# Attention rows scaled per head on ScalarE, GpSimd's joins and bias accumulations reordered, one Strassen level for one item's last factor

## The chip, the core and the metric

The kernel runs on one core of one Trainium2 chip. The metric is the device time of one execution in microseconds (us), and the value compared is the median of several runs. A profiled execution of the kernel before gives the timings by instruction; all times below that are not run times count from the start of its span.

The core has a matrix engine (TensorE, PE in the profile), three engines for elementwise work (VectorE = DVE, ScalarE = ACT, GpSimd = POOL) and a queue engine for transfers (SyncE = SP). Each engine works through its own instructions in order, and engines wait for each other by semaphores.

## What is computed

For each of 32 items `b`, with 512 nodes and 512 features, in float32:

```python
q, k, v = x @ Wq + bq, x @ Wk + bk, x @ Wv + bv          # 8 heads of 64
w       = softmax(q k^T / 8 + mask(adj))
x1      = layernorm(x + w v)
z       = norm_adj @ x1                                   # D^-1/2 adj D^-1/2
out     = layernorm(x1 + z @ W1 + b1)
```

The softmax is computed without subtracting the maximum, so that the division by the row sums can be made late: `yT` first holds the undivided `w v`, and is then multiplied, head by head, by `inv`, the reciprocal of the row sums.

## The kernel before, in words

**Tiling.** A node or feature axis of 512 is four tiles of 128 partitions. The products with the 512x512 weights are Strassen products: seven half-size products in place of eight. In most items, four of the seven are replaced by one more level, seven quarter-size products (`quarters_of`, called `leaf`), and the three others are `OUTER`. `seven` runs a table of products; every product accumulates in a PSUM region (A, B or D) and is moved out of it by a `put` or an `add` at the named steps. A later product into the same region has to wait until the earlier content has been read. In the leaf, `put` is a ScalarE copy and `add` a VectorE addition. For the attention's values, the target is tile `v`; for the graph convolution's second factor it is `y`.

**One item.** An iteration of the loop over `b` (line 874) runs four stages, and TensorE goes from one to the next without a gap in the program:

1. `stretch(b, one)`: scores, exponentials and value products of the first two head pairs. The 8 score tiles of 128x1024 use four PSUM pairs in turn, VectorE masks and moves each out (`e<-sc,maskT`), ScalarE takes the exponential, GpSimd adds the four tiles of a pair of heads to `acc` (`accumulate`). The value product of a pair is transposed by VectorE into the single buffer `yb`, and four SP transfers of 64 KB carry `yb` to `yT` (`unload_values`).
2. keys and queries of item `b+1` (`k0`, `k1`: 14 products). Beside it VectorE, ScalarE and GpSimd finish the convolution of item `b-2` and normalize item `b-1` (`measure`, `root`, `norm`, `low`).
3. `stretch(b, two)`: the other two head pairs.
4. A list of 27 pieces called `main` in line 949, numbered 0 to 26, for b from 1 to LAST-1 = 30: first factor of the convolution of item `b-1` (0 to 3), the leaf of the values of item `b+1` (4 to 10) and its `spread_last` (11), one outer product of the convolution (12), two steps of the outer products of the values (13), the leaf of the convolution (14 to 20), one outer step without a product (21), `spread_last` of `y` (22), and two outer products of each in turn (23 to 26).

**Order.** `play(main, beside)` writes out by hand which helper work follows which piece. All four compute engines keep that program order (`InOrder`); SP's transfers are not pinned. So a helper on an engine that waits holds all that is behind it there.

**Names that the change touches.** `inverse` makes `inv`; `scale` (line 606) is one VectorE multiplication of 128x512 per node tile with a broadcast `inv`; `grow` (668) multiplies the normalized rows of item `b-1` by `rdeg` on ScalarE; `combined` (779), called `join`, adds these rows to `y` on GpSimd; `residual` and `residual_bias` (673, 677) are GpSimd DMAs that add `x[b]` and `bv` to `yT`, 1 MB each; `lift` (664) adds `b1`; `second` (835) is the convolution's second factor with one level, seven half-size products, all moved out by VectorE. `stored[2]` holds `w1` in DRAM as it is before the quarter-size weights are written into it. `extend` is left for the last but one convolution.

Of the kernel before, what the change touches and what calls it, by code (L numbers as in the profile page):

```python
# [14 lines left out]
AF = mybir.ActivationFunctionType  # L15
# [4 lines left out]
H = 8  # L20
HD = 64
# [29 lines left out]
def unshifted(  # L51
# [14 lines left out]
    nc = tc.nc  # L66
# [32 lines left out]
    def each(f, *args):  # L99
        return [lambda a=a: f(*a) if isinstance(a, tuple) else f(a) for a in args]  # L100

    def run(pieces):
        for f in pieces:
            f()
# [155 lines left out]
    def swap(k):  # L260
        nc.sync.dma_start(wqv, stored[k])
# [202 lines left out]
    def accumulate(b, g):  # L464
        e = E[b, g]
        if b < LAST:
            a = work.tile([P, 2, N], F32, name="acc", bufs=2)
            gpsimd.tensor_add(a, e[0], e[1])
            for j in range(2, NT):
                gpsimd.tensor_add(a, a, e[j])  # L470
            ACC[b, g] = [a]
            return
        ACC[b, g] = []
        for l in range(2):
            n = 2 * ORDER.index(g) + l
            if n < 2:
                a = work.tile([P, 2, N], F32, name="acc", bufs=2)
            else:
                t, at = ((XT, 0), (XT, 2), (XT, 4), (wqv, 0), (wqv, 2), (wqv, 4))[n - 2]
                a = t[:, at : at + 2].rearrange("p k u o -> p k (u o)")  # L480
            gpsimd.tensor_add(a, e[2 * l], e[2 * l + 1])
            ACC[b, g].append(a)
# [26 lines left out]
                yb[32 * q : 32 * (q + 1)],  # L509
            )  # L510

    def stretch(b, gs, gap=()):
        banks("attention")
        for g in gs:
            scores(b, g)
        for g in gs:
            accumulate(b, g)
        banks("products")
        for g in gs:
            av = bank([P, N], "av")  # L520
            values(b, g, av)
            unload_values(b, g, av)
            if g == gs[0]:
                run(gap)
# [47 lines left out]
    def finish(b):  # L572
# [33 lines left out]
        def scale(i):  # L606
# [3 lines left out]
                t["inv"][:, i, :, None].to_broadcast([P, H, HD]),  # L610
            )

        def add(i):
            gpsimd.tensor_add(YT[b][:, i, :], YT[b][:, i, :], R[b][i])

# [57 lines left out]
        def residual():  # L673
# [7 lines left out]
            turn_values=[lambda: turn_values(ORDER[-1], bank([P, N]))],  # L681
            pairs=[[lambda i=i, g=g: add_pair(i, g) for i in all_] for g in ORDER],
            halves=each(root, (0, 2), (2, 2)),
            inverse=[inverse_all], scale=each(scale, *all_), add=each(add, *behind),
            measure=each(measure, *(all_ if b == LAST else behind)), root=[root],
            judge=[judge], norm=each(norm, *all_), low=each(low, *all_),
            lift=each(lift, *((3, 0, 1, 2) if b == LAST else behind)),
            grow=each(grow, *(all_ if b == LAST else behind)),
        )

    def convolve(b):
# [127 lines left out]
        def store(n, at):  # L819
# [11 lines left out]
            first=each(first, *range(DT)), block=each(block, *nodes), unload=each(unload, *range(DT)),  # L831
            parts=each(combine, *range(4)), quarters=each(quarter, *range(4)),
            leaf=quarters_of(left, w1, w1_quarters, lambda: t["whole"], begin), spread_last=spread_last,
            outer=seven(OUTER, multiply, put, add), join=each(combined, (0, 1), (1, 1), (0, 0), (1, 0)),
            second=seven(LATE_LOW if last else CHAIN, multiply, put, add), extend=extend,
            halves=[each(measure_half, *((n, i) for n in range(2))) for i in range(2)],
            measure=each(measure, *nodes), root=each(root, (0, NT)), store=each(store, *((n, 0) for n in nodes)),
# [36 lines left out]
    for b in range(B):  # L874
        one, two = ORDER[:2], ORDER[2:]
        f[b], c[b] = finish(b), convolve(b)
        ahead, back = f.get(b - 1), c.get(b - 2)
        if b == LAST:
            load_residual(b)
        stretch(b, one, (ahead["low"] if b == LAST else []) + (back["measure"][:3] if back else []))  # L880

        def folds(gs):
            return [[lambda g=g, b=b: fold(b, g)] for g in gs]

        def turns(b=b + 2):
            if b >= B:
                return [], [], []
            return [lambda: turn(b, 0)], [lambda: turn(b, 1)], [lambda k=k: combine(b, k) for k in range(4)]

        fold0, fold1 = folds(one) if b < LAST else ([], [])  # L890
        rest = back["measure"][3:] + back["root"] if back else []
        store = back["store"] if back else []
        if b < LAST:
            k0, k1 = keys_and_queries(b + 1, 0), keys_and_queries(b + 1, 1)
            main = [p for pair in zip(k0, k1) for p in pair]
            if b == 0:
                exact = each(compare, *range(NT))
                weights = each(lambda k: weigh_part(w1, gpsimd, k), *range(4))
                beside = {
                    1: fold0, 2: [degrees], 3: weights[:1], 4: fold1, 5: weights[1:2] + exact[:1], 6: exact[1:2],  # L900
                    7: weights[2:3], 8: exact[2:3], 9: weights[3:], 10: exact[3:], 11: [quarters],
                    12: each(lambda k: weigh_quarter(w1, w1_quarters, k, gpsimd), *range(3)),
                }
            else:
                measure, norm, low = ahead["measure"], ahead["norm"], ahead["low"]
                scale = ahead["inverse"] + ahead["scale"] if b == 1 else []
                beside = {
                    0: rest + scale + (ahead["add"] if b == 1 else []), 1: store[:1] + fold0, 2: store[1:2], 3: store[2:3] + fold1,
                    4: store[3:] + measure[:2], 5: measure[2:] + ahead["root"] + [quarters], 7: norm[:1] + ahead["judge"],
                    8: norm[1:2] + low[:1], 9: norm[2:3] + low[1:2], 10: norm[3:] + low[2:3],  # L910
                    11: low[3:] + ahead["lift_all"],
                }
            play(main, beside)
            if b == 0:
                nc.sync.dma_start(stored[2], w1)
        else:
            e = f[b]
            conv = c[b - 1]
            play(conv["first"], {
                0: rest + store[:1] + conv["parts"][:0], 1: store[1:2] + ahead["judge"] + conv["parts"][:1],  # L920
                2: store[2:] + e["sums0"],
                3: conv["parts"][1:] + e["inverse0"] + ahead["lift"] + ahead["grow"],
            })

        if b < LAST:
            swap(1)
        if b == LAST - 1:
            load_residual(b)
        stretch(b, two, f[b]["pairs"][0] + f[b]["pairs"][1] if b == LAST else ())

        fold0, fold1 = folds(two) if b < LAST else ([], [])
        turn0, turn1, combined = turns()
        if b + 2 < B:
            load_x(b + 2, 0)
            load_x(b + 2, 1)
        if b < LAST:
            end = f[b]
            leaf, spread_last, outer = values_of(b + 1)
            main = leaf + [spread_last]
            if b == 0:  # L940
                main += [lambda: run(outer[:2])] + outer[2:]
                play(main, {
                    1: fold0, 4: fold1, 8: turn0, 9: turn1 + combined[:2] + [lambda: weigh_quarter(w1, w1_quarters, 3, gpsimd)],
                    10: combined[2:] + [lambda: swap(0)],
                })
            else:
                conv = c[b - 1]
                other, join = conv["outer"], conv["join"]
                main = (
                    conv["first"] + main + other[:1] + [lambda: run(outer[:2])] + conv["leaf"] + other[1:2]  # L950
                    + [conv["spread_last"]] + outer[2:3] + other[2:3] + outer[3:] + other[3:]
                )
                grow, scale = ahead["grow"], end["scale"]
                parts = conv["parts"] + conv["quarters"]
                if b < LAST - 1:
                    beside = {
                        1: parts[:1] + fold0, 3: parts[1:] + fold1, 5: end["inverse"], 9: scale[:1], 10: scale[1:3],
                        12: scale[3:] + grow, 13: turn0 + turn1 + end["residual"] + combined[:1], 22: join[:1], 23: join[1:2],
                        24: join[2:3] + combined[1:2], 25: join[3:] + combined[2:], 26: end["residual_bias"] + [lambda: swap(0)],
                    }  # L960
                else:
                    measure, norm = end["measure"], end["norm"]
                    beside = {
                        1: parts[:1] + fold0, 3: parts[1:] + fold1, 5: end["inverse"], 9: scale[3:], 10: scale[:2],
                        12: scale[2:3] + grow + end["add"], 21: measure[:2], 22: join[:1], 23: join[1:2] + measure[2:] + end["root"],
                        24: join[2:3] + norm[:2], 25: join[3:] + norm[2:3],
                        26: norm[3:] + [lambda: nc.sync.dma_start(w1, stored[2])],
                    }
                play(main, beside)

# [311 lines left out]
```

## Time and profile before

| | |
|---|---|
| median of 3 runs | 2805.27 us (2803.79 to 2805.3) |
| the profiled execution's own time | 2805.72 us |
| its span, from first to last instruction | 2803.7 us, mean granted TensorE clock 0.997 |
| busy share of the span | PE 97%, DVE 76%, POOL 74%, ACT 47% |
| chain of work that ended last, by engine | PE 89%, DVE 8%, issue 2% |

One item in the middle of the run, from one start of stage 1 to the next, is 86.0 us. Its stages, with the time in each that the engines were busy:

| stage | from, to (us) | length | PE | DVE | ACT | POOL |
|---|---|---|---|---|---|---|
| 1, scores | 1322.80, 1330.70 | 7.90 | 7.83 | 7.15 | 4.30 | 7.47 |
| 1, values | 1330.70, 1337.80 | 7.10 | 7.07 | 6.27 | 4.14 | 6.94 |
| 2 | 1337.80, 1362.10 | 24.30 | 24.30 | 20.01 | 14.17 | 14.58 |
| 3 | 1362.10, 1376.20 | 14.10 | 14.10 | 9.86 | 9.30 | 9.21 |
| 4, pieces 0 to 3 | 1376.20, 1383.60 | 7.40 | 7.40 | 5.24 | 1.77 | 6.26 |
| 4, pieces 4 to 11 | 1383.60, 1390.40 | 6.80 | 6.80 | 3.78 | 2.35 | 5.64 |
| 4, pieces 12, 13 | 1390.40, 1393.85 | 3.45 | 3.45 | 3.45 | 3.04 | 3.37 |
| 4, pieces 14 to 20 | 1393.85, 1400.86 | 7.01 | 5.74 | 7.01 | 1.76 | 4.73 |
| 4, pieces 20 to 26 | 1400.86, 1408.83 | 7.97 | 7.97 | 3.80 | 0.59 | 6.17 |

A line of the timeline has the start, the length, the engine, the source line (L45 is the helper that records every pinned operation, so the tile names tell the work), the operation with output and inputs, the shape, the count, and in brackets the idle time of the engine before it and what ended that. `w` is `w1` and `w_quarters` its quarter-size parts; `e` is also the buffer in which the first factor of the convolution lies. For groups of instructions, times are means of single instructions; such a time includes latency, so back-to-back instructions of one kind can start at a shorter distance than their length.

### The profile page before, as it was taken

The numbers are of one execution on the slowest core, as the hardware profiler recorded it, in microseconds if no ns is written. First come the engines' busy times: TensorE is split into PE (matmuls) and PEld (weight loads), VectorE is DVE, ScalarE is ACT, GpSimd is POOL, SyncE is SP. The second block draws the span as 40 slices with busy tenths as digits, with TensorE's granted clock in tenths as the row PEclk, the third lists the DMA queues.
The fourth block names the chain that finished last, engine by engine and source line by source line (L and its number), as shares of the span: only waits on it lengthen the run. The fifth ranks groups of instructions, "written<-read, shape, count | busy, mean of one in ns | idle before, by whom it ended". The sixth has DMA issues, their size and how long they took to land.

```text
span 2803.7 us, 38312 instructions
## 1 busy us (share of the span) xinstructions
PE 2731.0 (97%) x14004; PEld 1929.7 (69%) x14004; DVE 2130.2 (76%) x2809; ACT 1329.1 (47%) x1927; POOL 2062.0 (74%) x1336
## 2 busy tenths in 40 slices
PE   9999999999999999999999999999999999999997
PEld 6677676676676766767767767667677676676664
DVE  4787777777877777777778777778777777777866
ACT  3345444445544454444554444554445444445543
POOL 5777767767777777777777777777867767767765
PEclk9999999999999999999999999999999999999998
DMA  6344545545445445454454554554544545545541
GB/s 181 112 106 102 130 101 135 119 103 129 118 104 124 113 113 124 100 132 122 100 134 108 119 123 100 128 123 100 127 121 102 130 100 135 121 102 129 132 106 35
DMA packets 419684, 325.30 MB, mean 116 GB/s; under 512 B 278432, under 2 KB 346016, under 8 KB 411168
## 3 DMA queue, kind: packets, MB, share of 16 engines
q1 hardware_dynamic: 370432, 226.04, 26.6%
q0 software_dynamic: 48048, 95.43, 21.6%
q8 instruction: 113, 1.85, 0.3%
q10 hardware_dynamic: 1008, 1.31, 0.2%
q14 instruction: 83, 0.68, 0.1%
HBM read 250.35 MB, written 39.06 MB: 103 GB/s over the span
## 4 chain that ended last, share of the span: by engine, by line
PE 89%; DVE 8%; issue 2%; POOL 0%; DMA 0%; ACT 0%; SPq 0%; DVEq 0%; POOLq 0%; ACTq 0%
PE mm L45 56%; PE sc L45 17%; PE av L45 16%; DVE yT L45 3%; DVE xT L45 2%; DVE y L45 1%; DVE v L45 1%; DMA yT<-yb 0%; DVE st L45 0%; DVE lo L45 0%; POOL yT L45 0%; DVE yb L45 0%; DMA xr<-in_x_dram 0%; ACT xT L45 0%; SPq L507 0%
## 5 line engine op out<-in xcount | busy, mean ns | idle before, releaser
L45 ACT ACTIVATE e<-e 128x1024 f32<-128x1024 f32 x512 | 539.5, 1057 | 369.1 <-DVE e L45 339.1
L45 DVE SCALAR_TENSOR_TENSOR e<-sc,maskT 128x1024 f32<-128x1024 f32 x512 | 585.0, 1216 | 90.8 <-PE sc L45 90.7
L45 POOL TENSOR_TENSOR acc<-acc,e 128x1024 f32<-128x1024 f32 x248 | 589.2, 2376 | 19.4
L45 PE MATMUL sc<-kq 64*128 64x512 f32 x2048 | 478.7, 605 | 0.5 <-ACT zT L45 0.4
L45 PE MATMUL av<-e,v 128*64 128x512 f32 x2048 | 456.2, 597 | 7.3 <-ACT e L45 4.3
L45 PE MATMUL mm<-xT,wk 128*128 128x256 f32 x1792 | 463.1, 381 | 0.0
L45 PE MATMUL mm<-xT,wqv 128*128 128x256 f32 x1792 | 459.9, 379 | 0.0
L45 POOL TENSOR_TENSOR acc<-e 128x1024 f32<-128x1024 f32 x126 | 297.0, 2357 | 156.4 <-ACT e L45 156.4
L45 POOL TENSOR_TENSOR xT<-xT 128x512 f32<-128x512 f32 x251 | 346.1, 1389 | 77.4 <-PE mm L45 41.1
L45 POOL TENSOR_TENSOR e<-e 128x512 f32<-128x512 f32 x244 | 331.6, 1370 | 75.5 <-ACT e L45 57.3
L45 PEld LDWEIGHTS mm<-xT,wk 128*128 128x128 f32 x1792 | 337.6, 190 | 69.8 <-DVE mv L45 23.5
L45 PEld LDWEIGHTS mm<-xT,wqv 128*128 128x128 f32 x1792 | 340.5, 190 | 46.3
L45 PEld LDWEIGHTS sc<-kq 64*128 64x128 f32 x2048 | 184.7, 186 | 262.6 <-issue 142.0
L45 PEld LDWEIGHTS av<-e,v 128*64 128x64 f32 x2048 | 158.3, 137 | 299.8 <-issue 223.9
L45 ACT ACTIVATE kq<-mm,bias 128x256 f32<-128x256 f32 x512 | 214.7, 473 | 288.9 <-PE mm L45 277.1
L45 PE MATMUL mm<-w,e 128*128 128x128 f32 (+1 forms) x1680 | 299.1, 321 | 37.3 <-DVE y L45 36.8
L45 PE MATMUL mm<-wqv,xT 128*128 128x128 f32 x1736 | 309.4, 322 | 2.5 <-DVE v L45 2.4
L45 PEld LDWEIGHTS mm<-w,e 128*128 128x128 f32 x1680 | 252.8, 191 | 61.6 <-issue 41.5
L45 DVE STREAM_TRANSPOSE yb<-av 128x512 f32<-128x512 f32 x127 | 91.1, 717 | 267.2 <-DMA yT<-yb 184.5
L45 PEld LDWEIGHTS mm<-wqv,xT 128*128 128x128 f32 x1736 | 262.2, 192 | 28.7 <-DVE v L45 3.1
L45 POOL TENSOR_TENSOR rstd<-ve,minus_half 128x4 f32<-128x4 f32 (+1 forms) x66 | 66.1, 1002 | 233.7 <-DVE nmu L45 230.8
L45 DVE TENSOR_TENSOR v<-v,mm 128x512 f32<-128x512 f32 x221 | 148.6, 685 | 83.6 <-PE mm L45 83.4
(140 smaller groups left out, 3523.1 us busy)
## 6 DMA issues: line engine op xcount, KB each, us to landing
wqv<-wv_parts SPq DMA_DIRECT2D x31, 1792.0 KB, 11.9
wqv<-wq_parts SPq DMA_DIRECT2D x30, 1792.0 KB, 7.1
yT<-yb SPq DMA_DIRECT2D x508, 64.0 KB, 2.4
e<-in_x_dram SPq DMA_DIRECT2D x248, 128.0 KB, 2.6
yT<-in_L_gnn_bias_dram POOLq DMA_DIRECT2D x30, 1024.0 KB, 14.5
out_dram<-y SPq DMA_DIRECT2D x120, 256.0 KB, 2.0
yT<-in_x_dram POOLq DMA_DIRECT2D x29, 1024.0 KB, 9.2
yT<-in_L_gnn_bv_dram POOLq DMA_DIRECT2D x29, 1024.0 KB, 9.5
```

The lines of the kernel that those rows point to most:

```text
L45: return self.tc.keep_in_program_order(op(*args, **kwargs))
```

## The change

- In items 1 to 29, the four VectorE multiplications of `scale` become 32 ScalarE activations of 128x64 (`scale_head`), placed in groups of 10, 10, 9 and 3 after pieces 6, 10, 16 and 20. `grow` moves from piece 12 to piece 20.
- In the same items, the GpSimd transfer `residual` moves from piece 13 to piece 22, and `residual_bias` from piece 26 to the next item's first stretch, between `accumulate` of its first and second head pair. The joins go in the order (0,0), (1,0), (1,1), (0,1) in place of (0,1), (1,1), (0,0), (1,0), the last of them after piece 24 in place of 25.
- In item 30, stage 4 computes the second factor of item 29's convolution with one level: `second` in place of leaf, outer products, `quarters`, `spread_last` and joins. Its list has 22 pieces. `w1` is read back from DRAM before stage 3 in place of after piece 26. `scale` (still on VectorE), `grow`, `add`, `measure`, `root` and `norm` of item 30 come earlier, and `low` and `lift` move into this list from the first stretch and from piece 3 of item 31.

```diff
-    def stretch(b, gs, gap=()):
+    def stretch(b, gs, gap=(), between=()):
...
         for g in gs:
             accumulate(b, g)
+            if g == gs[0]:
+                run(between)
...
+        def scale_head(i, h):
+            y = YT[b][:, i, ts(h, HD)]
+            scalar.activation(y, y, AF.Copy, scale=t["inv"][:, i, h : h + 1])
...
-            inverse=[inverse_all], scale=each(scale, *all_), add=each(add, *behind),
+            inverse=[inverse_all], scale=each(scale, *all_),
+            scale_heads=each(scale_head, *((i, h) for i in all_ for h in range(H))), add=each(add, *behind),
...
-            grow=each(grow, *(all_ if b == LAST else behind)),
+            grow=each(grow, *all_),
...
-            join=each(combined, (0, 1), (1, 1), (0, 0), (1, 0)),
+            join=each(combined, (0, 0), (1, 0), (1, 1), (0, 1)),
...
-        stretch(b, one, (ahead["low"] if b == LAST else []) + (back["measure"][:3] if back else []))
+        between = ahead["residual_bias"] if 1 < b < LAST else []
+        stretch(b, one, back["measure"][:3] if back else (), between)
...
-                3: conv["parts"][1:] + e["inverse0"] + ahead["lift"] + ahead["grow"],
+                3: conv["parts"][1:] + e["inverse0"] + ahead["grow"],
...
         if b == LAST - 1:
             load_residual(b)
+            nc.sync.dma_start(w1, stored[2])
         stretch(b, two, f[b]["pairs"][0] + f[b]["pairs"][1] if b == LAST else ())
...
+                if b < LAST - 1:
+                    main = (
...
                    )
+                else:
+                    second = conv["second"]
+                    main = (
+                        conv["first"] + main + second[:1] + [lambda: run(outer[:2])] + second[1:2] + outer[2:3]
+                        + second[2:3] + outer[3:] + second[3:]
+                    )
                 grow, scale = ahead["grow"], end["scale"]
-                parts = conv["parts"] + conv["quarters"]
+                parts, heads = conv["parts"], end["scale_heads"]
                 if b < LAST - 1:
                     beside = {
-                        1: parts[:1] + fold0, 3: parts[1:] + fold1, 5: end["inverse"], 9: scale[:1], 10: scale[1:3],
-                        12: scale[3:] + grow, 13: turn0 + turn1 + end["residual"] + combined[:1], 22: join[:1], 23: join[1:2],
-                        24: join[2:3] + combined[1:2], 25: join[3:] + combined[2:], 26: end["residual_bias"] + [lambda: swap(0)],
+                        1: parts[:1] + fold0, 3: parts[1:] + conv["quarters"] + fold1, 5: end["inverse"], 6: heads[:10], 10: heads[10:20],
+                        13: turn0 + turn1 + combined[:1], 16: heads[20:29], 20: heads[29:] + grow,
+                        22: end["residual"] + join[:1], 23: join[1:2],
+                        24: join[2:] + combined[1:2], 25: combined[2:], 26: [lambda: swap(0)],
                     }
                 else:
-                    measure, norm = end["measure"], end["norm"]
+                    measure, norm, low = end["measure"], end["norm"], end["low"]
                     beside = {
-                        1: parts[:1] + fold0, 3: parts[1:] + fold1, 5: end["inverse"], 9: scale[3:], 10: scale[:2],
-                        12: scale[2:3] + grow + end["add"], 21: measure[:2], 22: join[:1], 23: join[1:2] + measure[2:] + end["root"],
-                        24: join[2:3] + norm[:2], 25: join[3:] + norm[2:3],
-                        26: norm[3:] + [lambda: nc.sync.dma_start(w1, stored[2])],
+                        1: parts[:1] + fold0, 3: parts[1:] + fold1, 5: end["inverse"], 6: grow[:1],
+                        8: grow[1:2] + scale[3:], 9: grow[2:3] + scale[:1], 10: grow[3:] + scale[1:3] + end["add"],
+                        14: measure[:2], 15: measure[2:3], 16: measure[3:] + end["root"],
+                        17: norm[:1], 18: norm[1:2] + low[:1], 19: norm[2:3] + low[1:2],
+                        20: norm[3:] + low[2:3], 21: low[3:] + end["lift"],
                     }
```

More of the change, by code (lines that the diff above doesn't have):

```diff
@@ L833, in convolve @@
             leaf=quarters_of(left, w1, w1_quarters, lambda: t["whole"], begin), spread_last=spread_last,
-            outer=seven(OUTER, multiply, put, add), join=each(combined, (0, 1), (1, 1), (0, 0), (1, 0)),
+            outer=seven(OUTER, multiply, put, add), join=each(combined, (0, 0), (1, 0), (1, 1), (0, 1)),
             second=seven(LATE_LOW if last else CHAIN, multiply, put, add), extend=extend,
@@ L948, in unshifted @@
                 other, join = conv["outer"], conv["join"]
[L949 to L952, printed above, removed]
+                if b < LAST - 1:
+                    main = (
+                        conv["first"] + main + other[:1] + [lambda: run(outer[:2])] + conv["leaf"] + other[1:2]
+                        + [conv["spread_last"]] + outer[2:3] + other[2:3] + outer[3:] + other[3:]
+                    )
[4 more added lines that the diff above has]
+                        + second[2:3] + outer[3:] + second[3:]
+                    )
```

## The prediction

> **What bounds the kernel now.** TensorE is busy for 97% of the span (2731.0 of 2803.7 us), and 89% of the chain that ended last is PE. So only TensorE's gaps, and work slowed by late inputs, can be won. I read its waits first:
>
> ```profile
> PE mm L45 <- DVE y L45: 36.8, 29, 1.3
> ...
> PE av L45 <- ACT e L45: 4.3, 1, 4.3
> ```
>
> (total us, times, longest.) Half of the span's 72.7 us without PE is one wait of 1.27 us in each of 29 items. Its place, in TensorE's timeline of one item:
>
> ```profile
> 1398.53 1.06 PE L45 MATMUL mm<-w,e 128*128 128x128 f32 x8
> 1400.86 1.13 PE L45 MATMUL mm<-w,e 128*128 128x128 f32 x8 [1.27 <-DVE y L45]
> ```
>
> This is piece 20, the convolution leaf's last product; its PSUM region must first be read by VectorE. VectorE's timeline there:
>
> ```profile
> 1389.48 0.69 DVE L45 TENSOR_TENSOR v<-v,mm 128x512 f32<-128x512 f32 x1 [0.20 <-PE mm L45]
> 1390.09 6.58 DVE L45 TENSOR_TENSOR yT<-yT,inv 128x512 f32<-128x512 f32 x4
> 1396.59 0.68 DVE L45 TENSOR_TENSOR v<-v,mm 128x512 f32<-128x512 f32 x1
> 1397.19 2.36 DVE L45 STREAM_TRANSPOSE xT<-e 128x1024 f32<-128x1024 f32 x2
> 1399.48 1.84 DVE L45 TENSOR_TENSOR y<-y,mm 128x512 f32<-128x512 f32 x3
> ```
>
> The four scale multiplications hold everything up: the addition to `v` whose product was done at about 1394.0, the two transposes, and the additions to `y`.
>
> Next, the two score stretches of an item, which do equal work, and what VectorE does before the first:
>
> ```profile
> 1322.81 7.82 PE L45 MATMUL sc<-kq 64*128 64x512 f32 x32
> 1362.12 7.14 PE L45 MATMUL sc<-kq 64*128 64x512 f32 x32
> ```
> ```profile
> 1410.27 0.69 DVE L45 TENSOR_TENSOR y<-y,mm 128x512 f32<-128x512 f32 x1 [0.57 <-POOL y L45]
> ```
>
> From the scores' start to the value products it is 7.92 us (1322.81 to 1330.73) against 7.07 (1362.12 to 1369.19). The first stretch's masking starts 2.03 us after its scores (1322.81 to 1324.84), the second's 1.17 (1363.29), and the last score tiles wait for a PSUM pair. VectorE is late because its last addition waits for GpSimd's last join.
>
> Last, the end of the program:
>
> ```profile
> 2719.94 0.50 PE L45 MATMUL mm<-adjT,lo 128*128 128x512 f32 x1 [1.40 <-DVE lo L45]
> 2741.82 9.68 PE L45 MATMUL av<-e,v 128*64 128x512 f32 x32 [4.35 <-ACT e L45]
> ```
> ```profile
> 2735.09 4.97 POOL L45 TENSOR_TENSOR yT<-yT,b_r 128x512 f32<-128x512 f32 x4
> ```
>
> Item 31's exponentials lie on ScalarE behind `grow`, which waits for GpSimd's `lift`; before that, TensorE waited for `low`.
>
> [...] The scale rows agree: minimum 678 ns, median 1755 with GpSimd at work. I go by the trace's 6.5 us per item for what VectorE is freed of. [...] The one place where `yb` meets a bias accumulation agrees: eight transfers land in 2.3/4.1/7.1 us (least, median, most; item 30, 2650 to 2682), against 2.4 elsewhere:
>
> ```profile
> 2655.47 1.28 POOL L45 DMA_DIRECT2D wk<-in_L_gnn_bv_dram  x1 [3.04 <-PE sc L45]
> ```
> ```profile
> 2672.28 0.72 DVE L45 STREAM_TRANSPOSE yb<-av 128x512 f32<-128x512 f32 x1 [8.15 <-DMA yT<-yb]
> ```
>
> **The change, part by part.**
>
> *Scale on ScalarE (items 1 to 29).* Removed from VectorE: 6.5 us. The addition to `v` can then run at 1394.1 and the transposes end at 1397.1; the additions to `y` follow their products (ends near 1397.6, 1398.5, 1399.4), as those to `v` do in the other leaf without any PE wait. **The 1.27 us go: 29 x 1.27 = 36.8 us.**
>
> Added: 32 activations of 128x64. No row shows this shape. Four `grow` of 128x512 take 2.56 us and one 0.713, so they start 0.62 apart; two `kq` of 128x256 take 0.84 and one 0.473, 0.37 apart. That is 0.25 us and 1 ns per column, so 64 columns come every 0.19 to 0.3 us; without any overlap it would be 0.41 (0.713 less 448 columns at 0.67 ns, from the 1057 ns of 1024 columns). I take 0.29: groups of 2.9, 2.9, 2.6 and 0.9 us. The gaps in ScalarE's timeline: `inv` is ready at 1387.1 and the next copy due at 1390.6 (3.3 us); then until 1394.9 (3.8 us, freed of `grow`'s 2.56); from 1397.4 until about 1400.6 (3.2 us). All fit, so cost nothing. At 0.41 each group overruns, by up to 0.9 us.
>
> `grow` at piece 20 ends about 2.7 us before the next scores; join (0,0) needs its first two tiles, done 4.0 before.
>
> *Joins and `residual`.* Counted from the next scores' start, GpSimd's `y<-y` ends at -4.9 (1403.96, scores at 1408.83). Then `residual` (1.3) and four joins of 1.24: (1,1) ends at +0.1, (1,0) at -1.1. VectorE's last two additions, at piece 26, need these two and not the fourth join; their product ends at about +0.1. They run from +0.2 to +1.4, masking starts at +1.4 in place of +2.03. A PSUM pair is free three and four masks of 1.14 later, so the last tile waits no longer: **7.92 becomes 7.15, 29 x 0.77 = 22.3 us.** If GpSimd is a microsecond later, this gain is lost, no more.
>
> *`residual_bias` in the stretch.* GpSimd's `acc` then runs from +5.1 to +12.3, the DMA is issued until +13.6, and the second `acc` ends at +20.9 (20.0 before). Behind it wait `rstd` of item b-2, ScalarE's normalizations, and the copies of keys and queries between them. Its packets begin 2.4 us after issue (1326.72, DMA busy from 1329.1), at +14.7. The four `yb` transfers move from +12.8 to +15.8, so the fourth collides. Alternating with the 5.4 us of the accumulation it lands at about +20.5; `yb` is reused then, in place of +17.0. VectorE gets 1.3 us back, since the addition `ve` (1.51 us beside GpSimd's `acc`, 0.17 elsewhere) then runs alone: `nmu` is +22.5 in place of +20.1. With TensorE 0.77 earlier, ScalarE's copies are 3.2 us later against the pieces of stage 2; the ninth piece needs the copy that ended at 1348.68 and started at 1351.66, 3.0 us of cover. **I charge 0.3 us per item, 8.7 us**; bounds: 0, if the transfers just miss each other, and 1.8, if `yb` is a little later and `ve` no shorter. `residual` and `swap(0)` now overlap, as `lift_all` and `swap(1)` do (14.5 and 11.9 us to landing); used at +12.3 and +14.9, landed by about +9.6 and +10.4: nothing.
>
> *Items 30 and 31.* One level: ten pieces of 1.73 us in place of six (10.4) and a leaf of 6.55, +0.4 us on TensorE. GpSimd saves quarters and joins. Item 31 loses the `low` waits (1.4 and some 0.9 of pauses behind it), and its exponentials start behind `grow` alone, at about 2730.5. Value products then begin right after the scores, which are 2.3 earlier, and take 7.1: end near 2742 in place of 2751.5. **Gain 9.5**; I take 8, as VectorE is fuller in item 30. `w1`'s transfer is off the path if SP issues it when `w1` is free (about 2613); if it lies before `yb` in the queue it costs up to 6. I charge 1. Net 7.
>
> Sum: 36.8 + 22.3 - 8.7 + 7 = 57.4. The span becomes 2746.3, with the 2.0 us around it (2805.72 - 2803.7) 2748.3; that execution was 0.45 above the median shown, so **2748**.
>
> **Rivals.**
> 1. *No collision and all gains*, 36.8 + 22.3 + 9.5 = 68.6: 2737. For it: the overlap is only about a microsecond. Chance 0.20.
> 2. *ScalarE becomes the late one*: 0.41 us per head delays a copy that frees the leaf's first region, 0.9 us per item, and the joins. Gain 0.4 + 0.4 per item, 29 x 0.8 + 7 = 30: 2775. Against it: every shape of the trace overlaps its neighbour by 0.1 us. Chance 0.12.
> 3. *Slower*: the accumulation takes `yb`'s place as the bound of stage 2. It decides once `yb` frees later than about +22.6: of each us of delay over the 3.0 of cover TensorE loses one, and at 5.3 of delay (+20.5 is 3.2) the 2.04 us won per item and the 7 at the end, 0.24 per item, are gone. At a stall of 2.6 per item: 29 x (2.04 - 2.6) + 7 = -9: 2814. For it: item 30 shows `yb` held 8.15 us and TensorE stalled 1.9 behind it. Against: three transfers were in flight there. Chance 0.10.
>
> Forecast's own case 0.58, 2742 to 2765. **Range 2735 to 2785**: it takes in rivals 1 and 2 and a collision of up to 1 us per item. About 0.2% (5.6 us) is what can be told from no change: faster 0.88, within it 0.02, slower 0.10.
>
> **What would show it.** PE's wait for DVE `y` gone from its waits; the first score stretch at 7.1 to 7.2 us; no `av<-e` wait near the end; heads starting under 0.3 us apart; landing of `yT<-yb` with a maximum near 7 us in most items. A PE wait for ACT `kq` of over 2 us in stage 2 would make the prediction wrong, and so would a new wait for ACT `y` in the leaf.

## The result and the profile after

The changed kernel takes 2849.93 us (median of 6 runs, 2844.58 to 2858.17) against 2804.25 us for the kernel before (6 runs): a ratio of 1.0164, 95% interval 1.0145 to 1.0183. It is slower by 1.6%, where 2% faster was forecast.

The profiled execution took 2853.71 us. First the wait of TensorE that is largest in total (total us, times, longest), then the span and the granted clock, which was 0.997 before:

```profile
PE mm L45 <- ACT kq L45: 69.3, 29, 4.0
```
```profile
core 0: 2851.6 us, clock 0.984
```

The wait for VectorE's `y`, 36.8 us before, is gone. In its place stands a longer one, for ScalarE's copies of keys and queries in stage 2. TensorE's timeline of one item shows both, and one thing more:

```profile
1339.07 2.17 PE L45 MATMUL mm<-w,e 128*128 128x128 f32 x16
...
1348.07 7.18 PE L45 MATMUL sc<-kq 64*128 64x512 f32 x32
1355.34 7.09 PE L45 MATMUL av<-e,v 128*64 128x512 f32 x32
...
1375.42 1.03 PE L45 MATMUL mm<-xT,wqv 128*128 128x256 f32 x4
1379.20 1.89 PE L45 MATMUL mm<-xT,wk 128*128 128x256 f32 x4 [2.75 <-ACT kq L45]
1380.88 1.91 PE L45 MATMUL mm<-xT,wqv 128*128 128x256 f32 x4
1382.58 1.13 PE L45 MATMUL mm<-xT,wk 128*128 128x256 f32 x4
```

Pieces 19 and 20 of stage 4 run through without a gap, and the scores give way to the value products after 7.27 us (7.92 before). Both forecast gains are there. But in stage 2 TensorE waits 2.75 us, and the groups after the wait start 1.7 us apart in place of 0.86. The table by windows says why. Its columns are the window, its length, the busy time and instructions of PE, PEld, DVE, ACT and POOL, the granted clock, the DMA share and GB/s:

```profile
1378.00:1379.00 1.00, 0.00 (x0) 0.00 (x0) 0.96 (x4) 1.00 (x4) 0.00 (x0) 1.00 0.46 176
1379.00:1380.00 1.00, 0.80 (x2) 0.68 (x3) 0.96 (x3) 1.00 (x4) 0.00 (x0) 0.68 0.68 262
1380.00:1381.00 1.00, 1.00 (x4) 0.80 (x3) 0.96 (x3) 0.48 (x2) 0.00 (x0) 0.50 0.39 152
1381.00:1382.00 1.00, 1.00 (x4) 0.82 (x3) 0.93 (x5) 0.00 (x0) 0.39 (x1) 0.50 0.36 127
1382.00:1383.00 1.00, 1.00 (x4) 0.80 (x4) 0.96 (x4) 0.03 (x1) 0.92 (x3) 0.61 0.00 0
```

After the wait TensorE is granted half its clock for some 3.4 us (1379.4 to 1382.8). The chain that ended last (start, length, what) leads from that wait back to its cause, in the same item:

```profile
1360.56 0.62 SPq L507
...
1361.92 9.40 DMA yT<-yb
...
1371.54 0.72 DVE yb L45
...
1373.33 1.03 POOL rstd L45
...
1375.38 0.82 ACT kq L45 x2
```

A 64 KB transfer out of `yb`, 2.4 us before, takes 9.4. It meets the bias accumulation, which GpSimd now issues at that moment:

```profile
1360.39 1.29 POOL L45 DMA_DIRECT2D yT<-in_L_gnn_bv_dram  x1
```

VectorE's next transposition into `yb` waits for it, and with it all that is behind on VectorE; `rstd` on GpSimd waits for VectorE, a normalization on ScalarE for `rstd`, and the copies that TensorE needs lie behind that normalization. In all 29 items whose accumulation was moved, this `rstd` stands 3.1 to 5.6 us waiting for VectorE's `nmu`; so GpSimd itself, with its issue and its sums, is not the last to be ready.

### The profile page after: what moved, and what is told of

It is laid out like the page before. It is cut to its first block, busy times and chain, and to the rows that moved or that the text cites. A ratio compares the mean times of both kernels' runs of the same rounds, so it can differ in the third digit from the quotient of the medians.

```text
span 2851.6 us, 39174 instructions
## 1 busy us (share of the span) xinstructions
PE 2751.2 (96%) x13980; PEld 1958.7 (69%) x13980; DVE 1917.2 (67%) x2693; ACT 1547.7 (54%) x2851; POOL 2012.3 (71%) x1327
## 4 chain that ended last, share of the span: by engine, by line
PE 63%; POOL 15%; DMA 8%; issue 5%; ACT 4%; DVE 3%; SPq 1%; POOLq 0%; DVEq 0%; ACTq 0%
PE mm L45 44%; PE sc L45 10%; PE av L45 10%; DMA yT<-yb 8%; POOL acc L45 5%; POOL y L45 4%; POOL xT L45 3%; ACT kq L45 2%; ACT y L45 1%; SPq L507 1%; POOL yT L45 1%; POOL rstd L45 1%; DVE yb L45 1%; DVE st L45 1%; DVE y L45 1%
## 5 line engine op out<-in xcount | busy, mean ns | idle before, releaser
L45 PE MATMUL mm<-xT,wk 128*128 128x256 f32 x1792 | 485.3, 395 | 69.3 <-ACT kq L45 69.3
L45 PE MATMUL mm<-xT,wqv 128*128 128x256 f32 x1792 | 476.8, 390 | 0.0
L45 PE MATMUL sc<-kq 64*128 64x512 f32 x2048 | 459.1, 597 | 0.0
L45 PEld LDWEIGHTS mm<-xT,wk 128*128 128x128 f32 x1792 | 347.7, 197 | 153.3 <-issue 81.8
L45 POOL TENSOR_TENSOR xT<-xT 128x512 f32<-128x512 f32 x250 | 355.6, 1493 | 103.2 <-DVE xT L45 98.1
L45 PEld LDWEIGHTS mm<-xT,wqv 128*128 128x128 f32 x1792 | 352.9, 197 | 51.9
L45 POOL TENSOR_TENSOR acc<-e 128x1024 f32<-128x1024 f32 x126 | 312.0, 2481 | 99.8 <-ACT e L45 99.8
L45 POOL TENSOR_TENSOR e<-e 128x512 f32<-128x512 f32 x240 | 302.9, 1272 | 75.1 <-ACT e L45 57.3
```

Source lines behind the costliest of these rows:

```text
L45: return self.tc.keep_in_program_order(op(*args, **kwargs))
```

## The experiments

Four questions: is it the packets, the issue on GpSimd or ScalarE's 32 activations; is it the single buffer; what is each gain worth alone; and was the bias accumulation moved needlessly? The kernel before was timed anew beside each group of runs, so the reference differs a little.

### The bias accumulation left out

```diff
-        between = ahead["residual_bias"] if 1 < b < LAST else []
+        between = []
```

> The changed kernel without the accumulation of bv onto yT for items 1 to 29 (that addition is left out). Theory A (the bias accumulation's packets share the DMA engines with the four yb transfers and hold the yb buffer, which makes TensorE wait for ScalarE's copies and then run at half its clock for some 3 us): no PE wait for ACT kq, yT<-yb lands in at most 2.5 us, clock back to 0.997, about 2738 us. Theory B (ScalarE is late by itself, through the 32 activations per item): the wait for ACT kq stays, about 2850. Theory C (GpSimd's issue of 1.3 us and its later sums are the cause, not the packets): also about 2738 here, so C is told apart by the next kernel.

Measured: 2737.01 us against 2803.48, ratio 0.9763 (0.9747 to 0.9779). No PE wait for ACT `kq`; the clock is 0.998. VectorE's waits for the buffer, first in this kernel and then in the changed one:

```profile
DVE yb L45 <- DMA yT<-yb: 182.0, 46, 8.3
```
```profile
DVE yb L45 <- DMA yT<-yb: 384.2, 57, 10.6
```

Theory B falls: all activations are still there, and TensorE's 29 waits for ACT `kq` are gone. So the accumulation costs 2849.93 - 2737.01 = 113 us in its new place, 3.9 us in each of 29 items, and the rest of the change gains 66.5 us. A and C both fit.

### The accumulation issued after the second pair's sums

```diff
         for g in gs:
             accumulate(b, g)
-            if g == gs[0]:
+            if g == gs[1]:
                 run(between)
```

> The changed kernel with the bias accumulation issued after the sums of the second head pair in place of the first: GpSimd's issue of 1.3 us still lies ahead of rstd, but its packets start some 7 us later, when the first four yb transfers have landed. Theory A: the wait for ACT kq goes or stays under 0.5 us per item, the clock stays at 0.997, 2738 to 2750 us; the statistics of yT may wait 1 to 2 us for the landing, inside VectorE's slack of 3. Theory C (the issue on GpSimd): no better than the changed kernel, about 2850. Theory B: about 2850.

Measured: 2826.35 us, ratio 1.0080 (1.0063 to 1.0096), which none of the theories had. The first half of A holds: `yT<-yb` lands in at most 2.4 us in the item looked at, and there is no wait for ACT `kq`. C falls with it, since the issue still lies ahead of `rstd` on GpSimd. (The second buffer, below, says the same: there the issue stands where the change put it.) But another wait has come, in the timelines of VectorE and TensorE:

```profile
1368.17 0.69 DVE L45 BATCH_NORM_STATS2 st<-yT 128x6 f32<-128x512 f32 x1 [5.08 <-DMA yT<-in_L_gnn_bv_dram]
```
```profile
1375.30 1.10 PE L45 MATMUL mm<-xT,wk 128*128 128x256 f32 x4 [1.38 <-DVE kq L45]
```

The statistics of `yT` are the accumulation's consumer. Issued at 1358.12, the accumulation lands 10 us later; VectorE stands 5.08 us in place of the expected 1 to 2, with the additions to `kq` behind the statistics in its order. In all items TensorE waits 58.0 us for DVE `kq`, and the mean granted clock is 0.990. Neither of the two places tried, between the transfers that it disturbs and the statistics that need it, is free in the present order; the places between were not tried.

### The accumulation moved, in the kernel before

The parameter `between` and its value are those of the change:

```diff
...
+            if g == gs[0]:
+                run(between)
...
-                        24: ..., 26: end["residual_bias"] + [lambda: swap(0)],
+                        24: ..., 26: [lambda: swap(0)],
```

> The kernel before with nothing changed but the place of the bias accumulation: between the sums of the first and the second head pair of the next item. Theory A: yb is freed some 6 us later, TensorE waits about 2 us for ACT kq in every item and loses some 1.7 us more at half clock, on top of the 1.27 us wait that stays: 2890 to 2915 us. Theory C: the 1.3 us of issue are covered by 3.0 us, 2804. Theory B (the 32 activations): 2804.

Measured: 2883.26 us, ratio 1.0280 (1.0263 to 1.0297). TensorE's waits:

```profile
PE mm L45 <- ACT kq L45: 59.3, 29, 3.2
PE mm L45 <- DVE y L45: 36.8, 29, 1.3
```

The new wait stands beside the old one, without one activation of the change. It is a little shorter than in the changed kernel (2.04 us each against 2.39), and the move costs 80 us in place of 113. B and C had 2804. The time fell 7 us short of A's range: only 6 stretches of half clock follow these waits (mean granted clock 0.993), where A had one after each.

### A second buffer for the second pair

```diff
-        yb = work.tile([P, 4, NT, 32], F32, name="yb", bufs=1)
+        if b < LAST and g == ORDER[1]:
+            yb = NUM[:, 0, 0].rearrange("p (l i s) -> p l i s", l=4, i=NT)
+        else:
+            yb = work.tile([P, 4, NT, 32], F32, name="yb", bufs=1)
```

`NUM` is the buffer of the exponentials; its first slot has been consumed by the value product and the sums of the first pair when the second pair is transposed. All else is the changed kernel.

> The changed kernel with a buffer of its own for the second head pair's transposed values in the first stretch (a slot of the exponentials that is free by then), so that the transposition no longer waits for the first pair's transfers. The bias accumulation stays where the change put it, and its packets still meet the transfers. Theory A (what costs is the wait for the one yb buffer): the waits DVE yb <- DMA yT<-yb and PE <- ACT kq go, landing of yT<-yb stays long (up to 10 us), 2737 to 2745 us. Theory D (the slow transfers cost by landing late, whatever the buffer): still over 2800.

Measured: 2737.14 us, ratio 0.9759 (0.9746 to 0.9773), with the whole computation in place. That is the fastest of the kernels that compute everything. The transfers, with count, size and median us to landing; `yT<-e` are those from the new buffer:

```profile
yT<-in_L_gnn_bv_dram POOLq DMA_DIRECT2D x29, 1024.0 KB, 10.5
yT<-yb SPq DMA_DIRECT2D x384, 64.0 KB, 2.4
yT<-e SPq DMA_DIRECT2D x124, 64.0 KB, 5.7
```

VectorE's transposition, 1371.54 with 9.40 us of waiting before, now follows its product at once:

```profile
1310.67 0.72 DVE L45 STREAM_TRANSPOSE e<-av 128x512 f32<-128x512 f32 x1 [0.41 <-PE av L45]
```

The collision is still there: in this item the four transfers from `yb` land in 2.4 to 9.6 us. It costs nothing that the time shows, because nobody waits for `yT` so early. What cost the time was the wait for the one buffer. D falls. The second buffer and the moved accumulation in the kernel before:

> The kernel before with the bias accumulation moved (2883 us by itself) and the second buffer. Theory A: the 80 us vanish, 2798 to 2806 us. Theory D: stays near 2880.

Measured: 2804.09 us, ratio 0.9996 (0.9988 to 1.0005). The 80 us are gone.

### The gains one by one

Scale back on VectorE at pieces 9, 10 and 12, without the bias accumulation:

```diff
-                        ..., 5: end["inverse"], 6: heads[:10], 10: heads[10:20],
-                        13: turn0 + turn1 + combined[:1], 16: heads[20:29], 20: heads[29:] + grow,
+                        ..., 5: end["inverse"], 9: scale[:1], 10: scale[1:3], 12: scale[3:],
+                        13: turn0 + turn1 + combined[:1], 20: grow,
```

> The changed kernel without the bias accumulation (as in the run of 2737 us), with the scale back on VectorE at pieces 9, 10 and 12. If the 1.27 us wait is the scale's, it returns: 29 x 1.27 = 37 us more, 2774. If joins and residual had removed it too: 2737.

Measured: 2773.75 us, ratio 0.9891 (0.9876 to 0.9906), so 36.7 us more than 2737.01 (35.5 if each of the two is first taken from its own time of the kernel before). TensorE's wait is back as it was:

```profile
PE mm L45 <- DVE y L45: 36.2, 29, 1.3
```

The joins in the old order, also without the bias accumulation (the tuple of `join` alone is put back):

> The changed kernel without the bias accumulation, with the joins in the order of before. Join (1,0) is then the fourth on GpSimd, behind residual, ends at about +1.3 us after the scores' start, and masking starts at +2.0 in place of +1.4: up to 29 x 0.77 = 22 us more, 2752 to 2759. If the order doesn't matter: 2737.

Measured: 2773.87 us, ratio 0.9890 (0.9875 to 0.9905): 36.9 us (35.6 by the same count), more than expected, and by another way. The timelines of VectorE and TensorE:

```profile
1311.40 0.69 DVE L45 TENSOR_TENSOR y<-y,mm 128x512 f32<-128x512 f32 x1 [2.70 <-POOL y L45]
```
```profile
1312.14 1.99 PE L45 MATMUL mm<-w,e 128*128 128x256 f32 x8 [0.78 <-DVE y L45]
```

In the old order join (0,1) is GpSimd's first. It is now behind `residual` and `grow`, and VectorE's addition to the same region, after piece 24, comes after it in the program. So that addition waits, and TensorE's piece 26 for it, 0.78 us and 22.8 us in all; the additions of piece 26 are late in turn, and the first scores take 7.51 us in place of 7.27, 7 us in all. The rest was not traced. The change's order puts (0,1) last, behind VectorE's addition. So the new order belongs to the later `grow` and `residual`; whether it gains anything without them was not tried.

The last two items alone: the kernel before, with items 1 to 29 in the old order.

> The kernel before with only the change of the last two items (one level, norms, low and lift earlier, w1 read back earlier). Predicted gain 7 us: 2797, between 2794 (9.5 us) and 2803 (if the fuller VectorE of item 30, or w1's transfer ahead of yb, takes it back).

Measured: 2792.95 us, ratio 0.9963 (0.9949 to 0.9977): 10.5 us, more than the best case of 9.5. The exponentials of item 31 follow `grow` directly (ScalarE), and TensorE's value products follow the scores without a wait:

```profile
2724.17 2.56 ACT L45 ACTIVATE yT<-yT,rdeg 128x512 f32<-128x512 f32 x4
2726.64 8.25 ACT L45 ACTIVATE e<-e 128x1024 f32<-128x1024 f32 x8
```
```profile
2723.41 7.20 PE L45 MATMUL sc<-kq 64*128 64x512 f32 x32
2730.55 7.09 PE L45 MATMUL av<-e,v 128*64 128x512 f32 x32
```

SP reads `w1` back at 2612.2, as soon as its last reader is done (TensorE, whose last product with it starts at 2611.8), and TensorE has no new wait there.

### The bias accumulation back in its old place

```diff
-        between = ahead["residual_bias"] if 1 < b < LAST else []
+        between = []
...
-                        24: join[2:] + combined[1:2], 25: combined[2:], 26: [lambda: swap(0)],
+                        24: join[2:] + combined[1:2], 25: combined[2:], 26: end["residual_bias"] + [lambda: swap(0)],
```

> The changed kernel with the bias accumulation back at piece 26, directly behind residual's move to piece 22. Both write yT, so GpSimd must wait for residual's landing (issued 4.9 us before the scores, 13.5 us to landing, so until about +8.6) ahead of the issue, and holds its sums: acc of the first pair from +9.9 in place of +5.1, rstd not before +24.4 in place of +20.1. Packets from about +11.5 meet the yb transfers as well. Expected a PE wait for ACT kq of about 2 us per item and, with half clock, 2800 to 2840 us: moving residual late is what takes the bias accumulation's old place away. If GpSimd's wait were hidden: 2737 to 2745.

Measured: 2847.19 us, ratio 1.0153 (1.0135 to 1.0172), above the expected range but of the expected kind. GpSimd waits for `residual`, and `yb` is still held, in this item for 6.21 us. It is GpSimd that comes last here: its sums end and `rstd` follows at once, 2.3 us after `nmu` was ready. GpSimd's lines, then VectorE's:

```profile
1353.86 1.30 POOL L45 DMA_DIRECT2D yT<-in_L_gnn_bv_dram  x1 [4.07 <-DMA yT<-in_x_dram]
```
```profile
1364.79 4.80 POOL L45 TENSOR_TENSOR acc<-acc,e 128x1024 f32<-128x1024 f32 x2
1369.53 1.03 POOL L45 TENSOR_TENSOR rstd<-ve,minus_half 128x4 f32<-128x4 f32 x1
```
```profile
1367.08 0.15 DVE L45 TENSOR_SCALAR nmu<-mv 128x4 f32<-128x4 f32 x1
```

No `rstd` of the 29 items waits for `nmu` in this kernel. So the old place is no longer free, and for a reason of its own: the late activations make `residual` late, GpSimd stands waiting for it, and all that is behind it on GpSimd is late too. A second buffer would not take that wait away; the two together were not tried.

## Why the prediction was wrong

**What held.** The scale on ScalarE: the 1.27 us wait went, 36.7 us as against 36.8. The activations start 0.25 us apart (the trace has ten in 2.50 us), inside the 0.19 to 0.3 bracketed and not the 0.41 of rival 2. Masking's earlier start brought 0.65 us per item (7.92 to 7.27), not 0.77. The last two items brought 10.5 us, not 7. Together 36.8 + 18.9 + 10.5 = 66.2; measured without the bias accumulation, 66.5. That the kernels freed of the wait come out at rival 1's 2737 us to the microsecond is in part luck: its gains sum to 68.6 and were taken from 2805.27, where 66.5 came off 2803.48.

**The step that failed** is "*`residual_bias` in the stretch*", charged at 0.3 us per item. It measured 3.9. The mechanism was named there and in rival 3: the accumulation holds `yb`, and what is behind VectorE is late. The cover of 3.0 us was right too. The end of `nmu` in the kernel before and in the changed one:

```profile
1342.78 0.16 DVE L45 TENSOR_SCALAR nmu<-mv 128x4 f32<-128x4 f32 x1
```
```profile
1373.16 0.16 DVE L45 TENSOR_SCALAR nmu<-mv 128x4 f32<-128x4 f32 x1
```

That is +20.1 and +25.2 from the scores' start (1322.81 and 1348.07). With TensorE 0.65 us earlier in stage 2 the delay is 5.8, and 5.8 - 3.0 is 2.8; TensorE waited 2.75. One term was too small and one was missing:

- *The length of the accumulation.* I estimated its packets at 5.4 us. By the trace's packet records the first of its 2048 B packets came 2.2 us after the issue, at +14.5, as I had it, but the last one ended at 1370.62, 8.1 us later (7.6 is the median of the 29 items). Even in the kernel before, where the accumulation met no transfer from `yb`, it took 7.1 us (the median of 29). From 1365 to 1367 the changed kernel's records have packets of the two kinds one for one, 74 per us of each, where the `yb` transfers alone had some 800 per us just before 1362.5. So the third and fourth transfer could not end ahead of the accumulation, and `yb` was free at +23.5 (1371.54 - 1348.07), not at +20.5.
- *The clock.* It was in no term. Up to the end of stage 2 of item 30 the trace has 20 stretches of half clock, 75 us in all, at or just behind the end of these waits; taking half of that as lost gives an estimate of 38 us. With the wait's 69.3 that is 107 us, of the 116 us between the two profiled executions (2853.71 - 2737.33); the rest was not traced. The kernel before showed it in item 30: in its wait of 1.89 us and behind it, with the granted clock third from the end of the line:

```profile
2676.00:2677.00 1.00, 0.04 (x1) 0.00 (x0) 0.96 (x2) 0.59 (x1) 1.00 (x2) 1.00 0.62 99
...
2680.00:2681.00 1.00, 1.00 (x7) 1.00 (x6) 0.00 (x0) 0.23 (x1) 0.92 (x2) 0.50 0.03 8
```

I quoted the wait in rival 3 and did not read on.

The range left rival 3 out, at a chance of 0.10, and without the clock even rival 3 ended at 2814. Its low chance rested on "three transfers were in flight there". But in item 30 the other two had landed by 2664.5 and 2665.9, and for the rest of the 8.15 us only the accumulation's packets and those of `yb` ran, as here.

**Point by point of what was to show it:** PE's wait for DVE `y` gone, yes; first scores near 7.2 us, yes (7.27); no `av<-e` wait at the end, yes; heads under 0.3 us apart, yes; longest landing of `yT<-yb` near 7 us, no: 8.4 to 10.8 us in the 29 items. Of the two signs named for a wrong prediction, a wait for ACT `y` in the leaf did not come; a PE wait for ACT `kq` came in all 29 items, over 2 us in 22 of them, 2.39 us on average.

## What to carry to other kernels

A transfer that is moved is costed by what shares the DMA engines with it at its new time (here 9.4 us in place of 2.4 for a transfer of 64 KB), and by who waits for the *buffer* of the disturbed transfer, not only for its data: here data with some 45 us of slack (landed at 1371.3, first read by a scale activation at 1416.5) stalled the kernel through one single-buffered tile. Moving work off a loaded engine moves its consumers too: follow each of them to the queue it lands in. And a wait is not priced by its length alone if the matmul clock drops behind it, as here for 3.4 us behind 2.75 us of waiting; read the lines after the wait, once, in the trace one has.

## What the runs showed of the hardware

**Half clock behind some of TensorE's waits.** The changed kernel's trace has half clock at or just behind the end of 20 of TensorE's 29 waits for ACT `kq`, for 3.4 us each and 6.8 us in two cases. These 20 waits were 1.93 to 3.97 us long, the nine others, without it, 1.47 to 2.47 us. So the length alone does not tell them apart: one of 2.29 us at 1730.6 brought none, and one of 2.25 us at 1554.2 did, from 1556.9 to 1560.3, which at half of 3.4 us is an estimated 1.7 us more. In the run with the accumulation moved in the kernel before, one of 3.24 us, up to 503.8, brought none: the groups behind it start 0.86 us apart. In the kernel before, no half clock stands behind any of the 29 waits of 1.27 us, and the mean granted clock was 0.997. The changed kernel's runs also spread by 14 us, 2.4 us for the kernel before; whether the clock is the reason was not tried.
